# Routed experts visited once each, with half blocks and nested conditions, in a GNN and mixture-of-experts stack

## The chip, the cores and the metric

The kernel runs on one core of a Trainium2 chip. The core has a tensor engine (PE, with its weight loads shown apart as PEld), a vector engine (DVE), a scalar engine (ACT), GpSimd (POOL) and a sync engine (SP), each with an instruction queue of its own. The metric is the device time of one execution in microseconds, taken as the median of some runs. The kernel before took 1725.51 us (three runs, 1724.1 to 1725.95).

## The reference

The input is x, 625 nodes of 512 features, and a list of 10000 edges. Four graph layers alternate with four feed-forward layers, each added to x after a layer norm. Two of the feed-forward layers, called L1 and L3 here, are routed: each node picks two of eight experts, and only these two count in its sum. Cut to what matters:

```
# L1: 512 -> 1024 -> 512, with biases
logits = x @ gate_w + gate_b
vals, idx = top_k(logits, 2);  w = softmax(vals)
out = sum over the two experts e:  w_e * (relu(x @ w1[e] + b1[e]) @ w2[e] + b2[e])

# L3: 512 -> 1536 -> 512, gated
probs = softmax(x @ router_w.T)
gates, idx = top_k(probs, 2);  gates = gates / sum(gates)
out = sum over the two experts e:  gates_e * ((silu(x @ w1[e].T) * (x @ wgate[e].T)) @ w2[e].T)
```

So 1250 pairs of node and expert are computed in each of the two layers. All is float32. On the inputs of this case the experts get these numbers of nodes: in L1 96, 346, 175, 23, 54, 50, 350, 156, and in L3 197, 240, 352, 99, 77, 43, 149, 93.

## The kernel before

The whole stack is one straight program, scheduled by the order in which it is written: each engine takes its instructions in that order, and semaphores hold one behind another. x stays in on-chip memory as five groups of 125 nodes. The change touches the two routed layers and one place ahead of L1.

A routed layer starts with the logits. `top2` finds the two experts of each node as one-hot rows. `dispatch` (from L514) turns these into a list of places: matmuls with a triangle of ones give each pair its rank within its expert and each expert its total; a chain of small DVE instructions makes from rank and total a block number and a place in the block; one-hot matrices (`ohp` for the place, `ohb` for the block) ten matmuls then write the node of each place, and ten more its weight. There are NB = 17 blocks of B = 128 places: the first eight hold the first 128 nodes of each expert, the other nine ("overflow") hold what is left of the experts with more, in order. Empty places point to spare rows behind the nodes.

`routed` (from L621) runs over the blocks. `fetch` (L667) gathers a block's 128 rows of x by an indirect DMA on POOL's queue, two blocks ahead, into one of three buffers. `enter` (L674) transposes them on PE. `ahead` does the up matmuls of one chunk of 512 hidden features (L1170 in L1, L1335 in L3; 4 matmuls a weight chunk, each two instructions of 512 columns), `turn` (L688) transposes the hidden rows back, `back` (L697) multiplies by the down weights, scales by the weight of each place (L703) and adds the rows into `sums` in HBM by an indirect DMA (L705) on POOL. L1 has two chunks a block, L3 three. `run` orders them in a pipeline over the units (block, chunk) of all blocks: the up matmuls of the next unit stand between a unit's up matmuls and its turn, and its down matmuls come a unit later, across the border of two blocks as well. The eight base blocks are one such run; each overflow block is a run of its own, inside nested conditions `n_over > i`, so that after the first condition that fails all that follow are jumped over. The last thing in a run is the turn and the down matmuls of its last two units; the transposes of the next block (`enter`) stand ahead of these.

Weights come as chunks of 1 MB (128 x 2048 float32), four an expert in L1 and nine in L3, over a ring of eleven buffers on SP's queue (`bring`, `refill`, L206 and L730): as soon as a buffer has been read, the load of the chunk that is eleven further is issued. An overflow block loads its expert's chunks again, at an address that SP reads from the list of owners, under the condition that the block exists.

`fill` is a list of small pieces of work that `run` puts in, three a unit: in L1 the matmuls of the second bias (`expert_bias`, L479 and L486), the copy of x into `sums` (`keep`), and `normalise`, which makes the normalised adjacency for L2 out of the degrees with some 25 DVE instructions. L3 has only `keep`.

## Time and profile before

| what | value |
|---|---|
| median of three runs | 1725.51 us |
| the profiled execution: time, span | 1723.04 us, 1721.1 us |
| mean granted clock of PE | 0.936 |
| PE, DVE, ACT, POOL busy | 89%, 39%, 21%, 14% of the span |
| L1 routed: logits start, first up matmul, last down matmul ends | 771.3, 793.8, some 1018 us |
| L3 routed: softmax of the logits starts, first up matmul, last down matmul ends | 1259.9, 1282.2, some 1708 us |
| blocks run | L1: 8 and 6 overflow; L3: 8 and 5 overflow |
| bytes on SP's weight queue (q1) | 214.80 MB |

The columns of a row of instructions are: line, engine, operation, result and operands with the program's names and sizes, the number of instructions; busy time in all and mean length in nanoseconds of one; the idle time of the engine just before them, and what ended most of it. The chain is the work that ended last, followed back from the end. A row by stretches has, for each engine, busy time and number of instructions, then PE's granted clock as a share of full speed, the share of the DMA engines and the GB/s moved. Matmuls are pipelined, so the length of one is more than the distance to the next.

### The profile page before, as it was taken

To read this page: it belongs to the slowest core of one execution; us is meant where nothing else is said; L and a number is where in the kernel's file an instruction comes from. 1 tells how busy PE (TensorE), PEld (TensorE's weight loads), DVE (VectorE), ACT (ScalarE), POOL (GpSimd) and SP (SyncE) were. 2 spreads that over 40 slices of the span, in tenths; PEclk is the share of its full clock that TensorE was granted. 3 is DMA by queue.
4 is the path that set the end of the run, shared out by engine and by line. 5 is a ranking of instruction groups with operands and counts; after the bars stand their busy time and mean duration, and the time that the engine had idled before them with its cause. 6 is when DMAs were issued, how large, how long until landed. Compare 5 with 4: busy or idle time off the path is not lost.

```text
span 1721.1 us, 15559 instructions
## 1 busy us (share of the span) xinstructions
PE 1528.4 (89%) x5642; PEld 861.3 (50%) x5642; DVE 676.1 (39%) x1738; ACT 357.8 (21%) x680; POOL 235.5 (14%) x254
## 2 busy tenths in 40 slices
PE   7996999989897989846999969698759999999997
PEld 5774466555555656533444436354534444444443
DVE  9824562451974168466122225635331111111110
ACT  1102362011661046311111115301211000000100
POOL 2010042010540034101111112001000000000000
PEclk8998999999999989977999989799869999999998
DMA  3000200011001100136889731011258888869871
GB/s 135 16 28 25 73 1 25 31 68 53 22 1 49 49 26 1 40 112 234 302 270 342 256 87 73 25 49 49 102 217 299 301 309 304 307 244 359 311 265 50
DMA packets 40142, 237.12 MB, mean 138 GB/s; under 512 B 4779, under 2 KB 4907, under 8 KB 14299
## 3 DMA queue, kind: packets, MB, share of 16 engines
q1 hardware_dynamic: 30705, 214.80, 33.7%
q0 software_dynamic: 6608, 15.99, 4.1%
q10 hardware_dynamic: 2746, 5.25, 1.0%
q8 instruction: 48, 0.79, 0.2%
q14 instruction: 35, 0.29, 0.1%
HBM read 246.11 MB, written 14.26 MB: 151 GB/s over the span
## 4 chain that ended last, share of the span: by engine, by line
PE 70%; DVE 12%; issue 10%; DMA 4%; ACT 2%; POOL 1%; SPq 0%; POOLq 0%; ACTq 0%; DVEq 0%
PE ps_mf L359 17%; PE ps_y L697 9%; PE ps_h L1335 9%; PE ps_mn L367 7%; PE ps_h L1170 5%; PE ps_s L796 4%; PE ps_eo L496 4%; PE ps_o L860 3%; DMA sumsL<-slots,node 3%; PE ps_p L839 3%; PE ps_tr L328 2%; DVE ln_st L277 1%; DVE s L802 1%; PE ps_t L688 1%; DVE dst L913 1%
## 5 line engine op out<-in xcount | busy, mean ns | idle before, releaser
L1335 PE MATMUL ps_h<-ring,xgT 128*128 128x512 f32 x624 | 274.8, 595 | 0.8 <-DVE xgT L226 0.8
L697 PE MATMUL ps_y<-ring,hT 128*128 128x512 f32 x536 | 239.2, 593 | 0.9 <-issue 0.9
L1335 PEld LDWEIGHTS ps_h<-ring,xgT 128*128 128x128 f32 x624 | 118.7, 191 | 147.9 <-issue 145.3
L697 PEld LDWEIGHTS ps_y<-ring,hT 128*128 128x128 f32 x536 | 97.6, 190 | 103.9 <-issue 103.0
L825 POOL TENSOR_SCALAR s<-s,rs 125x625 f32<-125x625 f32 (+4 forms) x120 | 103.2, 875 | 294.0 <-DVE rs L822 269.9
L705 POOL DMA_INDIRECT sumsL<-slots,node x27 | 42.6, 1578 | 469.3 <-DVE slots L703 358.6
L1338 ACT ACTIVATE g<-ps_h 128x512 f32<-128x512 f32 x39 | 23.3, 597 | 395.6 <-PE ps_h L1335 364.5
L1170 PE MATMUL ps_h<-ring,xgT 128*128 128x512 f32 x224 | 103.2, 609 | 2.1 <-ACT xgT L234 1.3
L807 ACT ACTIVATE s<-s,mn 125x626 f32<-125x626 f32 (+4 forms) x120 | 87.2, 743 | 49.3 <-DVE mn L802 49.1
L802 DVE CUSTOM_DVE_ANT_0 s<-ps_s,mask 125x626 f32<-125x626 f32 (+4 forms) x120 | 82.6, 718 | 29.0 <-PE ps_s L796 27.8
L796 PE MATMUL ps_s<-kT,qT 64*125 64x313 f32 (+4 forms) x416 | 86.4, 466 | 2.8 <-DVE mn L802 2.8
L328 PE MATMUL ps_tr<-ident,xn 125*128 125x125 f32 x140 | 30.2, 398 | 62.6 <-DVE ln_nb L300 49.1
L226 DVE COPY hT<-ps_t 128x512 f32<-128x512 f32 x26 | 18.0, 692 | 171.5 <-PE ps_t L688 171.5
L1340 DVE TENSOR_TENSOR h<-ps_h,g 128x512 f32<-128x512 f32 x39 | 26.8, 686 | 147.9 <-ACT g L1338 147.9
L839 PE MATMUL ps_p<-ident,s 125*125 125x125 f32 x432 | 65.8, 293 | 14.0 <-POOL s L825 11.7
L359 PE MATMUL ps_mf<-xT,w 128*128 128x313 f32 x256 | 69.7, 434 | 6.6 <-ACT xT L402 6.6
L839 PEld LDWEIGHTS ps_p<-ident,s 125*125 125x125 f32 x432 | 53.9, 194 | 40.0 <-POOL s L825 28.6
L1170 PEld LDWEIGHTS ps_h<-ring,xgT 128*128 128x128 f32 x224 | 43.6, 196 | 57.5 <-issue 53.8
L817 DVE SCALAR_TENSOR_TENSOR s<-s,cnt 125x626 f32<-125x626 f32 x80 | 67.3, 863 | 9.9 <-ACT s L807 9.9
L496 PE MATMUL ps_eo<-w,h 128*125 128x512 f32 x160 | 70.6, 592 | 0.0
L860 PE MATMUL ps_o<-pT,v 125*64 125x375 f32 (+2 forms) x448 | 60.1, 413 | 9.0 <-DVE mn L802 4.2
L916 PE MATMUL ps_a<-dst,src 125*128 125x313 f16 x400 | 58.0, 309 | 6.9 <-DVE dst L913 5.3
(345 smaller groups left out, 1994.8 us busy)
## 6 DMA issues: line engine op xcount, KB each, us to landing
ring<-in_weights SPq DMA_DIRECT2D x195, 1024.0 KB
w<-in_weights SPq DMA_DIRECT2D x27, 1024.0 KB
rows_hbm<-xn ACTq DMA_DIRECT2D x2, 1120.0 KB
sumsL<-x ACTq DMA_DIRECT2D x2, 1120.0 KB
out<-sumsL SPq DMA_DIRECT2D x1, 1250.0 KB
x<-in_x SPq DMA_DIRECT2D x1, 1120.0 KB
x<-sumsL SPq DMA_DIRECT2D x5, 224.0 KB
rows<-in_rows SPq DMA_DIRECT2D x1, 1052.0 KB
```

The costliest lines, as they stand in the source:

```text
L359: nc.tensor.matmul(ps[:, half, :HC], w, r[:, half * HC:(half + 1) * HC], start=(n == 0), stop=(n == last))
L367: nc.tensor.matmul(ps[:T, 0, :width], src[:, k, t * T:(t + 1) * T], w[:, k, :width], start=(k == 0), stop=(k == KD - 1 and extra is None))
L496: nc.tensor.matmul(ps[:T, 0, :], h[:, t * T:(t + 1) * T], w, start=(f == 0), stop=(f == len(blocks) - 1))
L697: nc.tensor.matmul(ys[b][:, 0, :], hT[:, j, :], ring[n % RING][:, j, :], start=(c == 0 and j == 0), stop=(c == nch - 1 and j == 3))
L796: nc.tensor.matmul(ps[hh][:T, i, :w], qT[rr, b, t * T:(t + 1) * T], kT[rr, b, i * w:(i + 1) * w], start=True, stop=True)
L802: nc.vector.tensor_tensor_reduce(s[:, hh, :nb * w].rearrange("p (a c) -> p a c", a=nb), ps[hh][:T, :nb, :w], mask[:, t, :nb * w].rearrange ...
L807: nc.scalar.activation(s[:, hh, :nb * w], s[:, hh, :nb * w], AF.Exp, bias=mn[:, hh:hh + 1], scale=-1.0, accum_out=sm[:, hh:hh + 1] if caus ...
L825: nc.gpsimd.tensor_scalar(s[:, hh, :w], s[:, hh, :w], rs[:, hh:hh + 1], 1.0, op0=OP.mult, op1=OP.mult)
L839: nc.tensor.transpose(pp[:T, hh, j * T:(j + 1) * T], s[:, hh, j * T:(j + 1) * T], ident[:T, :T])
L860: nc.tensor.matmul(po[rr, 0, o:n * T], v[:, j, h * DH:(h + 1) * DH], pT[:, hh, j, o:n * T], start=(j == 0), stop=(j == nk - 1))
L1170: nc.tensor.matmul(ps[:, 0, :], xgT[:, k, :], w1[:, k, :], start=(k == 0), stop=(k == KD - 1))
L1335: nc.tensor.matmul(ps[:, i, :], xgT[:, k, :], w[i][:, k, :], start=(k == 0), stop=(k == KD - 1))
```

## The change

Experts are visited once each, in order, with no overflow list. The slots of an expert are now six (NL): slot 0 is a half block of 64 places, slots 1 to 5 whole blocks of 128. An expert whose number of halves (64 nodes, rounded up) is odd runs slot 0 for its first 64 nodes; then slot 1 runs if it has more than 64 nodes, and slots 2 to 5 in nested conditions. So NB is 48 for the places.

The half block (`Block` with l = 0) uses two column groups of the tensor engine: 64 nodes times the first half of the output columns go to the upper 64 rows of PSUM, the same nodes times the second half to the lower 64. Its result rows are added to `sums` as half rows, with their own list of places (`node2`, `gate2`).

Each block now runs its pipeline alone (`run`). Weights are loaded once an expert. The ring has twelve buffers; a refill during a block is issued under the condition that this block is the last of its expert, and every block of an expert starts from the same state of the ring. In L3 the order of an expert's chunks is up 0, gate 0, up 1, gate 1, down 0, up 2, gate 2, down 1, down 2, where before the three down chunks came last. The first twelve loads are issued ahead of the dispatch.

The rows of slots 1 and 0 of the next expert are gathered while one expert runs, into one buffer each (`fetch`, after `enter` has transposed the ones before); the rows of slots 2 and up go to a third buffer, and are transposed at the start of their block. Before expert 0, `enter(0)` and `enter(1)` stand one behind the other.

The dispatch has no thresholds, overflow numbers and owners; it has the totals, whether the halves are odd, and the start of the places. In L3 the softmax over eight is left out, and the two weights come from the difference of the two logits, as in L1. The bias matmuls of L1 move into the dispatch, behind the gather; their result is added to x there. `keep` follows the dispatch. `normalise` moves to the second layer of the graph layer ahead (two pieces after each evacuation of its projections).

The diff, cut to its core:

```diff
-TMORE = 3
+TMORE = 4
...
-NB = 17
-NO = NB - E
+NL = 6
+NB = E * NL
+BH = B // 2
...
-        for c in range(3):
-            w += [a[c], g[c]]
-        w += _chunks(i["L3_ffn_w2"][e].T)
+        d = _chunks(i["L3_ffn_w2"][e].T)
+        w += [a[0], g[0], a[1], g[1], d[0], a[2], g[2], d[1], d[2]]
...
+    def choose(lg):
+        m1, m2, o12 = top2(lg)
+        g12 = small.tile([T, 2, NT], F32, tag="g12", name="g12")
+        def weights12():
+            nc.vector.tensor_sub(g12[:, 1], m2, m1)
+            nc.scalar.activation(g12[:, 1], g12[:, 1], AF.Exp)
+            nc.vector.tensor_scalar(g12[:, 0], g12[:, 1], 1.0, None, op0=OP.add)
+            nc.vector.reciprocal(g12[:, 0], g12[:, 0])
+            nc.vector.tensor_mul(g12[:, 1], g12[:, 1], g12[:, 0])
+        return o12, g12, weights12
+    def dispatch(layer, lg, xg, bias=None):
...
+            weights12()
+            if bias is not None:
...
+            ci = dp.tile([P, E], I32, tag="ci", name="ci")
+            nc.vector.tensor_scalar(ci, tot, 1.0, float(BH - 1), op0=OP.max, op1=OP.add)
+            odd = dp.tile([P, E], I32, tag="odd", name="odd")
+            nc.vector.tensor_scalar(odd, ci, BH, None, op0=OP.bitwise_and)
+            base = dp.tile([P, E], F32, tag="base", name="base")
+            nc.vector.scalar_tensor_tensor(base, odd, -2.0, e768, op0=OP.mult, op1=OP.add)
...
-            gt = dp.tile([P, E, 4], F32, tag="gt", name="gt")
-            nc.vector.tensor_tensor(gt, tot[:, :, None].to_broadcast([P, E, 4]),
-                                    thr[:, None, :].to_broadcast([P, E, 4]), op=OP.is_gt)
-            nov = dp.tile([P, E], F32, tag="nov", name="nov")
-            nc.vector.tensor_reduce(nov, gt, axis=AX.X, op=OP.add)
-            pm = dp.tile([P, E, E], F32, tag="pm", name="pm")
-            nc.vector.tensor_mul(pm, before, nov[:, None, :].to_broadcast([P, E, E]))
-            ovb = dp.tile([P, E], F32, tag="ovb", name="ovb")
-            nc.vector.tensor_reduce(ovb, pm, axis=AX.X, op=OP.add)
-            delta = dp.tile([P, E], F32, tag="delta", name="delta")
-            nc.vector.scalar_tensor_tensor(delta, ovb, float(B), dconst, op0=OP.mult, op1=OP.add)
...
+            xg(node)
+            routing[layer] = number_of.rearrange("p a e -> p (a e)")
+            nc.vector.tensor_copy(number_of[:, 0, :], tot[0:1, :])
+            nc.vector.tensor_copy(number_of[:, 1, :], odd[0:1, :])
+            if bias is not None:
+                added = ktile("added")
+                for t in range(NT):
+                    if t % 2 == 0:
+                        pb = pstile("ps_eb")
+                    nc.tensor.matmul(pb[:T, t % 2, :], cT[:, t * T:(t + 1) * T], bias, start=True,
+                                     stop=True)
+                    nc.scalar.copy(added[:, t, :], pb[:T, t % 2, :])
 
...
+            firsts = dp.tile([P, 2, E], F32, tag="firsts", name="firsts")
+            for i, a in enumerate((node, gate)):
+                nc.vector.tensor_copy(firsts[:, i],
+                                      a.rearrange("p (e l) -> p e l", l=NL)[:, :, 0])
+            ps = pstile("ps_hf")
+            for g in range(2):
+                nc.tensor.matmul(ps[g * BH:(g + 1) * BH, 0, :2 * E], ident[:, :BH],
+                                 firsts.rearrange("p i e -> p (i e)"), start=True, stop=True)
+            node2 = small.tile([P, E], I32, tag="node2", name="node2")
+            nc.vector.tensor_scalar(node2, ps[:, 0, :E], 2.0, upper, op0=OP.mult, op1=OP.add)
+            gate2 = small.tile([P, E], F32, tag="gate2", name="gate2")
+            nc.vector.tensor_copy(gate2, ps[:, 0, E:2 * E])
+            if bias is not None:
+                for t in range(NT):
+                    nc.vector.tensor_add(x[:, t, :], x[:, t, :], added[:, t, :])
+        return node, gate, node2, gate2
...
+            rows_g = kpool.tile([P, NT, D], F32, tag="K", name="rows_g")
+            xg_half, xg_block, xg_more = rows_g[:BH, 0, :], rows_g[:, 1, :], rows_g[:, 2, :]
+            y_out = [rows_g[:, 3 + n, :] for n in range(2)]
+            xhT = [rpool.tile([P, KD, BH], F32, name=f"xhT{n}") for n in range(2)]
+            xbT = [rpool.tile([P, KD, B], F32, name=f"xbT{n}") for n in range(2)]
...
+            def refill(cond=None):
+                while brought["n"] < E * per:
+                    n = brought["n"]
+                    if n >= RING and n - RING not in read:
+                        return
+                    load(ring[n % RING], weights[w0 + n], cond)
+                    brought["n"] += 1
...
+            def fetch(e, node):
+                if e < E:
+                    gather(xg_block, node, e, 1)
+                    gather(xg_half, node, e, 0)
+            refill()
+            node, gate, node2, gate2 = dispatch(layer, lg, lambda node: fetch(0, node), bias)
+            _, numbers = nc.values_load_multi_w_load_instructions(routing[layer], min_val=0,
+                                                                  max_val=N)
+            counts, odd = numbers[:E], numbers[E:]
+            for part, hbm in by_node(sums[layer]):
+                nc.scalar.dma_start(hbm, x[part])
...
+            def turned(src, dst):
+                pt, n = pstile("ps_x"), src.shape[0]
+                for k in range(KD):
+                    nc.tensor.transpose(pt[:, 0, k * n:(k + 1) * n], src[:, k * P:(k + 1) * P],
+                                        ident[:n, :n])
+                evac(dst.rearrange("p k s -> p (k s)"), pt[:, 0, :KD * n])
+            def enter(e):
+                if e < E:
+                    turned(xg_block, xbT[e % 2])
+                    turned(xg_half, xhT[e % 2])
+                    fetch(e + 1, node)
...
+            class Block:
+                def __init__(self, e, l):
+                    self.e, self.l, self.h, self.hT = e, l, {}, {}
+                    n = 1 if l else 2
+                    self.parts = [(slice(g * B // n, (g + 1) * B // n),
+                                   slice(g * 512 // n, (g + 1) * 512 // n)) for g in range(n)]
+                    self.width = 512 // n
+                    self.xT = (xbT if l else xhT)[e % 2]
+                    self.cond = counts[e] < B * l + BH + 1 if l < NL - 1 else None
+                def done(self, i):
+                    read.add(self.e * per + i)
+                    refill(self.cond)
+                def ahead(self, c):
+                    ps, n = pstile("ps_h"), self.width
+                    for i, w in enumerate(up[c]):
+                        w = chunk_of(self.e, w)
+                        for k in range(KD):
+                            for rr, cc in self.parts:
+                                nc.tensor.matmul(ps[rr, i, :n], self.xT[:, k, :], w[:, k, cc],
+                                                 start=(k == 0), stop=(k == KD - 1))
...
+                def back(self, c):
+                    if c == 0:
+                        self.y = pstile("ps_y")
+                    hT, w, n, nj = self.hT.pop(c), chunk_of(self.e, down[c]), self.width, \
+                        self.width // P
+                    for g, (rr, _) in enumerate(self.parts):
+                        for j in range(nj):
+                            for ro, co in self.parts:
+                                nc.tensor.matmul(self.y[ro, 0, :n], hT[:, j, rr],
+                                                 w[:, g * nj + j, co],
+                                                 start=(c == 0 and g == 0 and j == 0),
+                                                 stop=(c == nch - 1 and g == len(self.parts) - 1
+                                                       and j == nj - 1))
+                    self.done(down[c])
+                    if c == nch - 1:
+                        if self.l == 0:
+                            i = self.e
+                            give(self.y[:, 0, :n], n, gate2[:, i:i + 1], by_half,
+                                 node2[:, i:i + 1])
+                        else:
+                            i = self.e * NL + self.l
+                            give(self.y[:, 0, :n], n, gate[:, i:i + 1], sums[layer],
+                                 node[:, i:i + 1])
+                def run(self):
+                    read.clear()
+                    read.update(before[0])
+                    brought["n"] = before[1]
+                    for n in range(nch + 2):
+                        if n < nch:
+                            self.ahead(n)
+                        if 1 <= n <= nch:
+                            self.turn(n - 1)
+                        if n >= 2:
+                            self.back(n - 2)
+            def more(e, l):
+                if l < NL:
+                    with tc.If(counts[e] > B * l - BH):
+                        turned(xg_more, xbT[e % 2])
+                        if l + 1 < NL:
+                            gather(xg_more, node, e, l + 1)
+                        Block(e, l).run()
+                        more(e, l + 1)
+            enter(0)
+            for e in range(E):
+                before = set(read), brought["n"]
+                enter(e + 1)
+                with tc.If(odd[e] > 0):
+                    Block(e, 0).run()
+                with tc.If(counts[e] > BH):
+                    gather(xg_more, node, e, 2)
+                    Block(e, 1).run()
+                more(e, 2)
...
-    normalise()
-    routed("L1", node, gate, 2, 1, l1_hidden, l1_turned,
-           expert_bias(comb, b2s[:E, 1, :]), fill)
+    routed("L1", lg, ((0,), (1,)), (2, 3), vec("L1_ffn_b1"), b2s[:E, 1, :])
...
-    pr = softmax8(node_logits(xnT, vec("L3_ffn_router_w"), None, "lg"))
-    m1, m2, o12 = top2(pr)
-    g12 = small.tile([T, 2, NT], F32, tag="g12", name="g12")
-    nc.vector.tensor_add(g12[:, 0], m1, m2)
-    nc.vector.reciprocal(g12[:, 0], g12[:, 0])
-    nc.vector.tensor_mul(g12[:, 1], m2, g12[:, 0])
-    nc.vector.tensor_mul(g12[:, 0], m1, g12[:, 0])
-    node, gate, whose = dispatch("L3", o12, g12.rearrange("p c t -> p (c t)"), W_L3, 9)
...
-    routed("L3", node, gate, 3, 2, l3_hidden, l3_turned)
+    lg = node_logits(xnT, vec("L3_ffn_router_w"), None, "lg")
+    routed("L3", lg, ((0, 1), (2, 3), (5, 6)), (4, 7, 8))
```

## The prediction

> **What bounds the kernel now.** I read the page's busy shares first, then the chain that ended last by stage, then the stretches between named instants. In the profiled execution (span 1721.1 us, time 1723.04; the median of the three runs is 1725.51, so its own sum gets 2.5 us more at the end) the tensor engine is the bound.
>
> ```profile
> PE 1528.4 (89%) x5642; PEld 861.3 (50%) x5642; DVE 676.1 (39%) x1738; ACT 357.8 (21%) x680; POOL 235.5 (14%) x254
> PE 70%; DVE 12%; issue 10%; DMA 4%; ACT 2%; POOL 1%; SPq 0%; POOLq 0%; ACTq 0%; DVEq 0%
> L1335 PE MATMUL ps_h<-ring,xgT 128*128 128x512 f32 x624 | 274.8, 595 | 0.8 <-DVE xgT L226 0.8
> L697 PE MATMUL ps_y<-ring,hT 128*128 128x512 f32 x536 | 239.2, 593 | 0.9 <-issue 0.9
> L1170 PE MATMUL ps_h<-ring,xgT 128*128 128x512 f32 x224 | 103.2, 609 | 2.1 <-ACT xgT L234 1.3
> q1 hardware_dynamic: 30705, 214.80, 33.7%
> q8 instruction: 48, 0.79, 0.2%
> ```
>
> The routed matmuls have almost no idle time: 0.8, 0.9 and 2.1 us in all. 624 up matmuls at 48 a block are 13 blocks in L3, 224 at 16 are 14 in L1: eight base blocks each, five and six overflow blocks. So a block less is its whole time gained, and any wait put on PE is its whole time lost. The stages, with columns PE, PE loads, DVE, ACT, POOL, clock, DMA share and rate:
>
> ```profile
> 794.00:925.00 131.00, 129.01 (x367) 61.46 (x368) 37.47 (x78) 18.33 (x45) 17.10 (x14) 0.98 0.86 298
> 925.00:1018.00 93.00, 92.05 (x266) 43.93 (x264) 21.32 (x63) 13.16 (x33) 15.50 (x12) 1.00 0.64 219
> 1282.00:1545.00 263.00, 262.85 (x705) 123.09 (x706) 31.61 (x48) 22.96 (x40) 17.60 (x14) 0.99 0.83 295
> 1545.00:1709.00 164.00, 163.42 (x441) 76.24 (x439) 21.11 (x31) 14.27 (x25) 12.91 (x10) 1.00 0.73 259
> ```
>
> Weights stream at 83 to 86% of the DMA engines while PE is full: a load is hidden only as long as nobody waits for all of them. From q1, 33.7% of 1721 us moves 214.80 MB, so a 1.05 MB chunk takes 2.83 us at full rate. The chain in L3 and at its start, and PE's first rows there (start, length, what, idle before):
>
> ```profile
> 1320.00 6.87 PE ps_h L1335 x16
> 1352.66 6.87 PE ps_h L1335 x16
> 1272.42 7.72 DMA slots<-rows_hbm,node
> 1280.28 1.09 PE L674 MATMUL ps_x<-ident,slots 128*128 128x128 f32 x4 [8.46 <-DMA slots<-rows_hbm,node]
> 1282.15 10.35 PE L1335 MATMUL ps_h<-ring,xgT 128*128 128x512 f32 x20 [0.78 <-DVE xgT L226]
> 793.79 5.33 PE L1170 MATMUL ps_h<-ring,xgT 128*128 128x512 f32 x8 [0.85 <-DVE xgT L226]
> 791.85 1.09 PE L674 MATMUL ps_x<-ident,slots 128*128 128x128 f32 x4 [4.57 <-DMA slots<-rows_hbm,node]
> 771.27 2.33 PE L421 MATMUL ps_lg<-xnT,lg_w 128*64 128x313 f32 x16 [0.63 <-ACT xnT L234]
> ```
>
> An L3 block is 1352.66 - 1320.00 = 32.7 us. A warm 8-matmul group takes 3.43 us (0.43 each), but 5.33 after the idle of 4.57, and 20 take 10.35 instead of 8.6 after 8.46: **an idle of some 5 us also costs about 1.8 us of slow clock** behind it. An idle of 0.8 does not.
>
> **The change, part by part.** Tokens per expert, from the reference's routing of these inputs: L1 96 346 175 23 54 50 350 156, L3 197 240 352 99 77 43 149 93. In halves of 64: L1 2 6 3 1 1 1 6 3, L3 4 4 6 2 2 1 3 2. After, L1 runs 9 full and 5 half blocks, L3 11 full and 2 half.
>
> *Half block.* Two 64-column groups replace one of 128. The row of L421 is the nearest: 64-wide, 313 columns, 16 matmuls in 2.33 us, 0.146 each, where one alone is 0.26 by the 0.43 of 512; two go side by side. So I take half of a full block (L3 16.4, L1 7.6); the bound on the other side is a whole one.
> 1. Blocks: L1 11.5 for 14, at 15.2 us: **-38**. L3 12 for 13: **-32.7**. This is all that the half blocks buy.
> 2. The expert-bias matmuls leave PE's path in L1 (0.7 + 1.98 + 2.77 us, with their waits and the gap of 1.28): **-6**; they now lie in the dispatch, in the gather wait (4.57 us idle today), and the cost is 0 to +3 if they overrun it. I take 0.
> 3. Shorter dispatch. L3 loses softmax8 (1259.92 to 1261.35, 1.4 us) and both lose a row of DVE steps of 0.14 to 0.23 us, but NB grows from 17 to 48, so ohb and gates lengthen: L3 **-3**, L1 0 (between -3 and +2).
> 4. The normalise steps (some 15 us of DVE) move out of L1's fill into layer 1's projections, where PE is full and DVE has room for two steps behind each 3.5 us group: 0, up to +5 if not.
>
> *What it adds on PE's path.*
> 5. Second gather. enter(1) stands ahead of expert 0's blocks on PE, but fetch(1) goes out on POOL only after enter(0) has read its buffer; before, three buffers let fetch(0) and fetch(1) go together. One more issue-to-landing per layer: 5.24 + transposes and evacuation, **+7.5** in L1; 7.72 in L3 with weights in flight, **+8** (bounds 5.2 and 10).
> 6. Blocks l=2 and up: gathered rows are transposed and evacuated at the block's start with nothing beside it: 0.7 to 0.9 evacuation idle, and an ACT table load (1.28 us) on the Relu/Silu alternation, some 1.8 each. L1 4, L3 4: **+7 and +7** (3 to 10).
> 7. Blocks no longer overlap their neighbours. In L1 (two chunks) the last turn waits for h (0.7) behind one 0.43 group, and back(0) for hT: 0.5 for each of 9 full, 1 for each of 5 half blocks, **+9.5**. L3 has a third chunk between: 0.
> 8. Entries are run for every expert, used or not: 8 half transposes, three unused whole ones: **+4 and +2**.
> 9. **The untaken half waits for the weights.** In the built program the skipped branch on SP brings its semaphores up to date by waiting for each load in flight, and PE's first matmul of the full block that follows waits for SP's bump, since the skipped half could have rewritten its ring slots. In L3 the last block of an expert issues nine loads; d0 is read only at 24.9 of 32.7 us, and five leave from there on: 25.1 + 5 x 2.85 + some 2 to land is 41, against a block end of 32.6. Less the entry transposes PE stands 8 us. e1 to e4: **+32**. Before, the same loads were hidden since they belonged to the next expert's third chunk. e5 (half only) reaches such chunks 3 us early, and its nine loads (26 us) outlast its visit, so e6 stands 11 us: **+14**. L1 loads four a visit; only e1 is caught: **+4**. Bounds: 0, if the wait is satisfied in time, and +50.
> 10. Short visits of L1's e3, e4, e5 (8.5 us): the next gather sits on POOL behind this expert's scatter-add (1.6 us issue, landing 6.6), then two gathers at 1 us and 5.3 to land, some 14 a round: **+11** (0 to 16).
> 11. Slow-clock restarts behind the idles of 5, 9 and 10: 4 in L1, 6 in L3 at 1.8: **+7 and +11**.
> 12. Skipped branches on PE, 14 in L1 and 15 in L3. Each drains PE's counter (matmul latency some 0.3 us) and jumps. Before, all Ifs that PE ran fell through, and cost nothing in the chain; the one skip per layer lies behind the last block, where POOL's next instruction came 0.1 us later. I take 0.7: **+10 and +10.5** (bounds 0.1 and 3, the latter if the code must be fetched).
>
> [...]
>
> Sum, L1: -38 - 6 + 7.5 + 7 + 9.5 + 4 + 4 + 11 + 7 + 10 = **+16**. L3: -32.7 - 3 + 8 + 7 + 2 + 32 + 14 + 11 + 10.5 = **+49**. The profiled execution becomes 1788, the median 1790 us.
>
> **Rivals.**
> A. *Faster: the skipped branch does not hold PE.* If the loads land before the skip's bump is wanted (item 9 nothing, 6 of the restarts gone) and skips cost 0.1: -50 - 11 - 18 on the sum, -14: **1711**. For it: DMA share 0.83, not 1, and fewer chunks in all (104 loads instead of some 170). Against it: nine loads of 2.83 need 25.5 us of 32.7, and five are bound to the tail. It decides when the stall per expert is under 1 us.
> B. *Code is fetched at each skip.* A small load lands in some 3 us (the 256 KB fills: 3.0), 29 skips at 3 instead of 0.7: +67, **1857**. For it: PE's program nearly doubles. [...]
> C. *Halves do not run side by side.* Five times 7.6 and two times 16.4: +71, **1861**. Against: L421.
>
> **How the numbers follow.** Sum as worked out 0.57 (own range 1755 to 1825); A with its partial forms 0.26; B 0.12; C 0.05. The range goes from 1702 (A with the gather chain of 10 hidden too) to 1850 (most of B). Within 0.2%, 3.5 us, which is also about what a measurement here can tell from no change, falls 0.04, from partial forms of A. Faster 0.22, slower 0.74.
>
> **What would show it.** Right: PE idle of 6 to 10 us before ps_h at e1 to e4 of L3, ended by a DMA of ring or by SP's queue; a second idle before ps_x at each stage's start; clock under 1 behind them; half blocks of 16 and 8 us; fewer bytes on q1 (some 140 MB). Wrong: L3's routed stretch (now 1282.15 to 1708.4, 426 us) under 400 says A; more than 480 with idle at skips ended by nothing named says B; ps_h rows of half blocks at 0.43 a pair of columns instead of 0.21 says C. The largest single doubt is item 9, then 12.

## The result, and the profile after

The changed kernel took 1797.82 us (median of four runs, 1795.88 to 1803.73) against 1725.12 us for the kernel before: 1.0427 times as long, 95% interval 1.0402 to 1.0453. The forecast was 1790 us, range 1702 to 1850, slower with a chance of 0.74. The profiled execution took 1799.03 us and its span was 1797.2 us, 76 us more than the span before. Below, e0 to e7 are the experts of a layer, and an expert that runs its half block alone (e3, e4 and e5 of L1, e5 of L3) is called half-only.

The page of the changed kernel, lines that answer to those of before (L761 are the up matmuls of both layers, L718 the transposes at an expert's entry):

```profile
PE 1512.9 (84%) x5966; PEld 861.8 (48%) x5966; DVE 671.3 (37%) x1697; ACT 382.2 (21%) x709; POOL 256.5 (14%) x275
...
q1 hardware_dynamic: 20769, 142.44, 21.3%
...
q8 instruction: 85, 1.39, 0.3%
...
L761 PE MATMUL ps_h<-ring,xbT 128*128 128x512 f32 x672 | 318.7, 633 | 62.1 <-SPq L847 40.2
...
L718 PE MATMUL ps_x<-ident,rows_g 128*128 128x128 f32 (+1 forms) x160 | 25.9, 302 | 40.6 <-PEq L836 25.8
```

PE works 15.5 us less than before, and the weight queue moves 72 MB less: 142 MB, where some 140 were forecast. But the up matmuls, which had 2.9 us of idle time ahead of them in all, now have 62, and the entry transposes 41. 40.2 of the first are ended by SP's queue at L847, the condition around the half block; 25.8 of the second by PE's own sequencer at L836, the condition around further blocks.

The stretch from first to last routed weight matmul of each layer, changed kernel (columns PE, PE loads, DVE, ACT, POOL, clock, DMA share, GB/s):

```profile
806.50:1035.90 229.40, 197.98 (x764) 98.41 (x764) 39.27 (x91) 27.63 (x78) 39.80 (x36) 0.92 0.42 130
1301.10:1783.70 482.60, 419.27 (x1288) 198.26 (x1288) 51.23 (x81) 61.45 (x85) 38.51 (x32) 0.92 0.42 148
```

The same stretches before:

```profile
793.80:1018.00 224.20, 221.26 (x631) 105.59 (x631) 58.99 (x141) 31.48 (x78) 32.81 (x26) 0.99 0.77 265
1282.10:1708.40 426.30, 426.25 (x1144) 199.33 (x1144) 52.08 (x77) 37.23 (x65) 30.42 (x24) 1.00 0.79 282
```

PE now stands 31 us in L1 and 63 in L3, and the mean clock of both stretches has fallen from 0.99 and 1.00 to 0.92.

Cut at the logits (first L421 of the layer), the first up matmul and the last down matmul, the whole difference is:

| stretch | before | after | difference |
|---|---|---|---|
| up to L1's logits | 771.3 | 772.5 | +1.2 |
| L1 logits to first up matmul | 22.5 | 34.0 | +11.5 |
| L1 weight matmuls | 224.2 | 229.4 | +5.1 |
| L1's end to L3's logits | 235.4 | 234.1 | -1.4 |
| L3 logits to first up matmul | 28.7 | 31.2 | +2.5 |
| L3 weight matmuls | 426.3 | 482.6 | +56.3 |
| rest | 12.7 | 13.5 | +0.9 |

L1 together is +16.6 (forecast +16), L3 +58.8 (forecast +49).

Who PE waited for in the two stretches of weight matmuls, changed kernel, L3 and then L1 (us in all, times, longest):

```profile
PE ps_h L761 <- SPq L847: 36.6, 4, 9.4
PE ps_x L718 <- PEq L836: 11.6, 4, 7.2
PE ps_h L761 <- PEq L847: 10.6, 2, 5.5
PE ps_h L761 <- ACT xbT L234: 4.1, 4, 2.0
PE ps_h L761 <- SPq L836: 3.3, 1, 3.3
...
PE ps_x L718 <- PEq L836: 14.2, 3, 7.8
PE ps_h L761 <- SPq L847: 3.6, 1, 3.6
```

Four waits for SP in L3, 36.6 us: these are e1 to e4, the forecast's item 9 (32 us). But 38.6 us in the two layers (11.6, 10.6 and 14.2 in these lines, and 2.2 before one ps_h of L1) are ended by PE's own sequencer, where the sum had 20.5 us for the skipped branches on PE (item 12). The place of the first wait for SP, at e1 of L3, PE's rows and then the instructions of line L847 there:

```profile
1370.81 0.59 PE L804 MATMUL ps_y<-ring,hT 128*128 128x512 f32 x1
1373.05 1.02 PE L718 MATMUL ps_x<-ident,rows_g 128*128 128x128 f32 x8 [1.64 <-PEq L836]
1382.66 2.04 PE L761 MATMUL ps_h<-ring,xbT 128*128 128x512 f32 x2 [8.60 <-SPq L847]
```

```profile
L847 SPq EVENT_SEMAPHORE  x8: 17/17/17, 1382.1 to 1382.6; - x8
L847 PEldq COMPARE_BRANCH  x1: 6470/6470/6470, 1373.2 to 1373.2; - x1
L847 DVEq COMPARE_BRANCH  x1: 63/63/63, 1374.1 to 1374.1; - x1
...
L847 PEldq EVENT_SEMAPHORE  x1: 51/51/51, 1379.7 to 1379.7; - x1
L847 SPq COMPARE_BRANCH  x1: 50/50/50, 1381.9 to 1381.9; - x1
```

SP comes to its branch only at 1381.9 and brings its semaphores up to date by 1382.6; PE goes on at 1382.66. That is the forecast wait. What SP did just before, from 1364 to 1384:

```profile
SPq L836 <- SPq L836: 9.6, 5, 3.7
```

So the waiting for loads is done at L836, in the skipped nest of further blocks of e0, and L847, the skipped half block of e1, passes the delay on in 0.7 us. But PE's own branch, which DVE does in 63 ns, takes **6470 ns** there. It lies under the wait for SP and is hidden by it. At e6 nothing hides it: there the rows of L836 have

```profile
L836 PEldq COMPARE_BRANCH  x1: 6598/6598/6598, 1682.6 to 1682.6; - x1
...
  PE ps_x L718: 7.2, 1
```

and PE stands 7.2 us. In the trace's DMA records two packets of 16 KB of the instruction queue q8 start at 1684.84 and 1686.11, inside this branch, two at 1375.48 and 1376.80 inside the one at e1, and one at 1298.27 inside a branch of 4.35 us at L3's start. Of PE's 80 branches in the two layers, 18 have such a packet inside, and they take 2.5 to 7.1 us; one takes 1.4 without; the other 61 take 0.07 to 0.44. So the long branches wait for code. Distance alone does not decide it: the jump over the half block of L3 takes 6.47 us at e1 and 0.35 at e3.

The half blocks do what they should. PE's rows for one in L1, and the start of a whole block behind it:

```profile
883.95 3.67 PE L761 MATMUL ps_h<-ring,xhT 128*64 128x256 f32 x32
887.56 0.44 PE L777 MATMUL ps_t<-ident,h 128*128 128x128 f32 x2
888.14 0.44 PE L777 MATMUL ps_t<-ident,h 128*128 128x128 f32 x2
888.51 3.67 PE L804 MATMUL ps_y<-ring,hT 128*64 128x256 f32 x32
892.12 3.27 PE L761 MATMUL ps_h<-ring,xbT 128*128 128x512 f32 x7
```

It takes 892.12 - 883.95 = 8.2 us, against the 15.2 of the forecast for a whole one.

### The profile page after: what moved, and what is told of

The parts are those of the page before. It is cut to its first block, busy times and chain, and to the rows that moved or that the text cites. A ratio compares the mean times of both kernels' runs of the same rounds, so it can differ in the third digit from the quotient of the medians.

```text
span 1797.2 us, 17215 instructions
## 1 busy us (share of the span) xinstructions
PE 1512.9 (84%) x5966; PEld 861.8 (48%) x5966; DVE 671.3 (37%) x1697; ACT 382.2 (21%) x709; POOL 256.5 (14%) x275
## 5 line engine op out<-in xcount | busy, mean ns | idle before, releaser
L761 PE MATMUL ps_h<-ring,xbT 128*128 128x512 f32 x672 | 318.7, 633 | 62.1 <-SPq L847 40.2
L761 PEld LDWEIGHTS ps_h<-ring,xbT 128*128 128x128 f32 x672 | 134.1, 204 | 227.2 <-issue 216.1
L804 PE MATMUL ps_y<-ring,hT 128*128 128x512 f32 (+1 forms) x664 | 209.8, 511 | 0.0
L804 PEld LDWEIGHTS ps_y<-ring,hT 128*128 128x128 f32 (+1 forms) x664 | 92.7, 169 | 92.2 <-issue 83.4
L733 POOL DMA_INDIRECT sumsL<-rows_g,node x27 | 43.1, 1598 | 581.2 <-DVEq L836 299.2
L769 DVE TENSOR_TENSOR h<-ps_h,g 128x512 f32<-128x512 f32 (+1 forms) x39 | 25.2, 647 | 249.3 <-ACT g L768 249.3
L694 POOL DMA_INDIRECT rows_g<-rows_hbm,node x52 | 50.3, 967 | 150.0 <-DVE gates L628 72.1
L732 DVE TENSOR_SCALAR rows_g<-ps_y,gate 128x512 f32<-128x512 f32 (+1 forms) x27 | 18.4, 681 | 137.0 <-PE ps_y L804 137.0
L359 PEld LDWEIGHTS ps_mf<-xT,w 128*128 128x128 f32 x256 | 49.5, 194 | 26.6 <-ACT xT L402 7.1
L718 PE MATMUL ps_x<-ident,rows_g 128*128 128x128 f32 (+1 forms) x160 | 25.9, 302 | 40.6 <-PEq L836 25.8
## 6 DMA issues: line engine op xcount, KB each, us to landing
x<-sumsL SPq DMA_DIRECT2D x5, 224.0 KB
```

The costliest lines, as they stand in the source:

```text
L359: nc.tensor.matmul(ps[:, half, :HC], w, r[:, half * HC:(half + 1) * HC], start=(n == 0), stop=(n == last))
L761: nc.tensor.matmul(ps[rr, i, :n], self.xT[:, k, :], w[:, k, cc], start=(k == 0), stop=(k == KD - 1))
L804: nc.tensor.matmul(self.y[ro, 0, :n], hT[:, j, rr], w[:, g * nj + j, co], start=(c == 0 and g == 0 and j == 0), stop=(c == nch - 1 and g = ...
```

## The experiments

Theory 1 is item 9 of the prediction: SP's skipped half block holds PE until the weights in flight have landed. Theory 2 came from the profile after: a taken branch on PE waits for its code. A theory 3 came later: both hold, and the loads in flight lengthen the fetch of code. The rivals are that the time lies in the work added around the blocks, and, for L1, that gathers come late (item 10). Times are medians; differences are to the changed kernel's 1797.8 us; ratios are to the kernel before on the same chip, whose medians on the chips used were 1724.4 to 1726.0 us.

### The half block behind the first whole block

```diff
-                with tc.If(odd[e] > 0):
-                    Block(e, 0).run()
                 with tc.If(counts[e] > BH):
                     gather(xg_more, node, e, 2)
                     Block(e, 1).run()
-                more(e, 2)
+                with tc.If(odd[e] > 0):            # now odd + (tot > 128)
+                    with tc.If(odd[e] > BH // 2):
+                        Block(e, 0).run()
+                    more(e, 2)
```

(and the condition of the loads, so that the last block of an expert issues them.)

> Same work, other order: the half block of an expert stands behind its first whole block, and the skips of half block and further blocks are joined where both are empty. Theory 1 (PE waits at e1 to e4 of L3 because SP's skipped half block first lets all weight loads land): the first chunks of an expert are no longer touched by a block that can be skipped just ahead of them, so the idles of 8.6, 9.4, 9.4 and 9.2 us go, e5 (half only) gets such a wait instead of its 3.3. Theory 2 (the taken branch on PE itself takes 3 to 7 us where its target must be fetched): most branches now stand behind the last matmuls of a block, which are queued ahead and cover them, so the idles of 5.5 at e0 and 5.1 at e7 go too. Both together: 45 to 55 us less than the changed kernel, some 1745 us. Rival (the time is in separate block pipelines and entries): under 10 us less.

1756.63 us, 41 less, where 45 to 55 were expected; ratio 1.0177 (1.0156 to 1.0199). Idle in L3's stretch fell from 63.3 to 31.9 us. The four waits for SP at e1 to e4 are gone, e5 has one of 9.1 as expected, and e7 one of 5.0 that was not expected. L1 did not gain (32.8 us idle): its half-only experts now jump over the whole block instead. The order alone takes back more than half of the loss. It does not tell theory 1 from 2, since both go with the order.

### A shorter nest

```diff
-NL = 6
+NL = 4
```

> Four slots an expert instead of six: the code that is jumped over behind an expert's last block shrinks from four whole blocks to two. On these inputs no expert has more than 352 nodes, so nothing is left out here; an expert with over 448 would lose nodes. Theory 2 (code fetch): the long branches behind L1's e3 and e4 (3.8 and 7.1 us) and L3's e5, e6 and e7 (6.6, 6.6 and 3.2) shorten by a page of code or go, 10 to 25 us less than the changed kernel. Theory 1 (weights landing) and the chain of gathers: nothing changes but 1 us of the dispatch.

1769.06 us, 29 less, where theory 2 had 10 to 25; ratio 1.0244 (1.0218 to 1.0270). No work that was done before is left out. L1's stretch went from 229.4 to 215.4 us: the idles before ps_x that PE's sequencer ended fell from 14.2 to 7.3. L3's went from 482.6 to 470.2; the waits for SP at e1, e2 and e4 stayed (8.8, 9.3 and 10.3 us), and the branch at L3's start too (4.1 us). The wait at e3 fell from 9.4 to 1.2 us, which neither theory had foreseen, and most of L3's gain is there. The trace has the reason: e2 of L3 has three whole blocks, and with four slots the third is the last, so that its loads carry no condition and no nest is skipped behind it. SP comes to L847 at 1549.0, 0.6 us after PE's last down matmul of e2; with six slots it came at 1575.9, 10.8 us after, from a skipped nest. PE goes on at 1550.9, and only at 1553.7 has SP seen the last load land. So the skipped half block alone does not hold PE until all loads have landed; the skipped nest ahead of it does. Code packets fell from 85 to 72. So L1's idle at its half-only experts goes with the code that is jumped over, and is not the chain of gathers of item 10, which this run leaves as it was.

### No loads from blocks

```diff
                 def done(self, i):
                     read.add(self.e * per + i)
-                    refill(self.cond)
```

> The loads that blocks issue are left out in both layers, so that only the first twelve chunks of a layer are loaded and later experts multiply by the wrong weights; every instruction on PE stays. Theory 1 alone: the idles before ps_h at L3's e1 to e4 fall under 1 us, and with them e5's 3.3, e6's 7.2 and L1's 3.6; some 60 to 70 us less. Theory 1 and 2: what is left is the branch, 6.5 to 7 us at e1, 5 at e2, 1 at e3, 5.5 at e4, and e6 stays at 7; some 25 to 30 us less.

1705.88 us (one run), 92 less, more than either theory allows. But L1's output is another one, so L3's routing is too, and L3 ran other blocks; only L1 can be read. There the wait for SP (3.6 us) is gone, the longest branch is 3.9 us instead of 7.1, and the stretch is 217.1 us instead of 229.4. The same was then done in L3 alone:

```diff
-                    refill(self.cond)
+                    if layer == "L1":
+                        refill(self.cond)
```

> As the run without loads from blocks, but in L3 alone, so that L1 computes the right thing and L3's routing is that of the reference; L3 multiplies by wrong weights from its second expert on. Idle inside L3's routed stretch is 63 us in the changed kernel. Theory 1 alone (weights landing): the waits of 8.6, 9.4, 9.4, 9.2 and 3.3 us fall under 1 us each, e6 and e7 too, 50 us of idle less and some 65 us of time. Theory 1 and 2 (a fetch of code at the branch of 3 to 7 us, whatever the loads do): 21 us of idle less, some 25 us of time. Theory 3 (both, and the weight loads lengthen the fetches, since both go through the DMA engines): branches of 3 to 4 us instead of 5 to 7, 35 us of idle less, some 40 us of time.

1752.70 us (one run), 45 less; idle in L3 went from 63.3 to 22.7 us. Of the three numbers that of theory 3, some 40 us less, is the nearest. At e1 PE's rows are now, with the branch of L848 (L847 of the changed kernel) behind them:

```profile
1374.09 1.02 PE L718 MATMUL ps_x<-ident,rows_g 128*128 128x128 f32 x8 [1.10 <-DVEq L837]
1376.77 3.61 PE L762 MATMUL ps_h<-ring,xbT 128*128 128x512 f32 x4 [1.67 <-ACTq L848]
```

```profile
L848 PEldq COMPARE_BRANCH  x1: 453/453/453, 1374.2 to 1374.2; - x1
```

Both waits have gone from this place, for SP and for code: 0.45 us instead of 6.47. Theory 1 is shown. Theory 3 can be read where both kernels fetch one packet at the same branch, the nest skipped behind the whole blocks of L3's e0, e1, e3 and e6. At e0, changed kernel and then this one:

```profile
L836 PEldq COMPARE_BRANCH  x1: 6969/6969/6969, 1365.3 to 1365.3; - x1
L837 PEldq COMPARE_BRANCH  x1: 3769/3769/3769, 1366.9 to 1366.9; - x1
```

At the four places the branch takes 6.6 to 7.0 us in the changed kernel and 3.4 to 3.8 here. By the DMA records the packet itself takes 0.9 to 1.4 us in both, but it starts 4.1 to 4.6 us after the branch there and 0.9 to 1.1 here. From e0's branch to its packet the DMA engines are 93% busy there, and 6% here. So at these places the fetch is longer with loads in flight. Whether a branch fetches at all is another thing: that of e1 above is free here with no change to PE's work, and the runs do not show why.

### The old order of L3's weights

```diff
-        w += [a[0], g[0], a[1], g[1], d[0], a[2], g[2], d[1], d[2]]
+        w += [a[0], g[0], a[1], g[1], a[2], g[2], d[0], d[1], d[2]]
...
-    routed("L3", lg, ((0, 1), (2, 3), (5, 6)), (4, 7, 8))
+    routed("L3", lg, ((0, 1), (2, 3), (4, 5)), (6, 7, 8))
```

> L3's chunks of an expert again in the order up, gate three times and then the three down chunks, as in the kernel before. Six loads instead of four leave before the down matmuls, so the last lands some 4 us earlier, about 37.5 us after the block's start instead of 41. Theory 1: the waits for SP at e1 to e4 fall from 9 to about 5 us each, but not under the length of the branch (6.5, 4.8, 0.4, 5.3 us) where theory 2 holds: 12 to 16 us less than the changed kernel. If the loads in flight are not what PE waits for: nothing.

1771.17 us, 27 less; ratio 1.0269 (1.0241 to 1.0297); the expectation was 12 to 16. The idles before e1 to e4 are 5.3, 7.1, 4.8 and 4.6 us where they were 8.6, 9.4, 9.4 and 9.2: 14.8 less, as worked out from the landing of the last load. The first, 5.3, is PE's branch (5.6 us) and not SP. What was not foreseen: e5's wait (3.3) and most of e7's (5.1 to 1.7) went too, and with less idle came less slow clock: the time on a lowered clock in L3's stretch fell from 74 to 43 us.

### Loads behind the expert, out of all conditions

```diff
                 def done(self, i):
                     read.add(self.e * per + i)
-                    refill(self.cond)
...
                 more(e, 2)
+                read.update(range(e * per, (e + 1) * per))
+                refill()
```

> The changed kernel with its weight loads taken out of the conditions: they are issued without a condition behind each expert, so no branch of SP has a load in it. All work is done with the right weights, and the order on PE is that of the changed kernel. Theory 1: nothing on PE can wait for SP's skipped branch any more, and in L3 the chunks still come in time, since the first of nine lands some 5 us after an expert's end and is read 10 us after it. Theory 2: what is left at L3's e1, e2 and e4 is the branch itself (6.5, 4.8 and 5.3 us), at e3 1 us, at e6 7. Some 20 to 25 us less than the changed kernel, about 1775, and by the weights alone (without theory 2) 1745 or less. If the loads, which now leave in one burst beside the branches, lengthen the fetches, the gain falls to 15.

1762.42 us, 35 less, where 20 to 25 were expected; ratio 1.0213 (1.0197 to 1.0229). All weights are loaded and used, and SP has no load in a condition. PE's waits in L3's stretch:

```profile
PE ps_h L760 <- PEq L846: 14.1, 2, 7.1
PE ps_x L718 <- PEq L835: 6.1, 1, 6.1
PE ps_h L760 <- DMA ring<-in_weights: 6.1, 3, 4.1
PE ps_x L718 <- DVEq L835: 5.5, 5, 1.1
```

None is for SP. So the waits of e1 to e4 were for SP's skipped blocks, and not for the weights themselves, which come in time for all but e5 and e6 (6.1 us). What is left is code: e3 and e4, where the branch over the half block now stands beside the burst of loads and takes 7.1 and 7.5 us, while e1 and e2 are free. The nests skipped behind the whole blocks of e0, e1, e3 and e6, where now no load is in flight, take 3.3 to 3.7 us.

### Whole blocks only

```diff
-            nc.vector.tensor_scalar(odd, ci, BH, None, op0=OP.bitwise_and)
+            nc.vector.tensor_scalar(odd, ci, 0, None, op0=OP.bitwise_and)
...
-                with tc.If(odd[e] > 0):
-                    Block(e, 0).run()
-                with tc.If(counts[e] > BH):
-                    gather(xg_more, node, e, 2)
-                    Block(e, 1).run()
+                gather(xg_more, node, e, 2)
+                Block(e, 1).run()
```

(with the conditions moved by half a block, and no gather or transposes for a half.)

> The change without its half blocks: an expert runs its first whole block without any condition and further ones under nested conditions, 14 blocks in L1 and 13 in L3 as before the change; no half block is gathered, transposed or jumped over. Blocks: +38 in L1 and +33 in L3 against the changed kernel. If theories 1 and 2 hold, what the jump over the half block costs goes with it: e0 5.5, e1 to e4 36.6, e5 to e7 some 12, slow clock behind these 15, L1 some 15, half entries 4: 88 less. Together some 15 to 20 us less than the changed kernel: the half blocks, as they are put in, cost more than they save. Rival (the half blocks earn their 71 us and the loss is elsewhere): 50 to 70 us more.

1756.72 us, 41 less; ratio 1.0177 (1.0160 to 1.0194); 15 to 20 less were expected. With 14 and 13 blocks again, L1's stretch is 236.2 us and L3's 440.5, and they are almost full:

```profile
803.50:1039.70 236.20, 218.42 (x610) 101.61 (x608) 42.42 (x91) 30.25 (x76) 39.59 (x35) 0.99 0.47 139
1300.80:1741.30 440.50, 427.79 (x1138) 197.44 (x1136) 52.23 (x77) 36.51 (x64) 36.81 (x30) 1.00 0.46 162
```

```profile
PE ps_x L717 <- DVEq L834: 6.6, 6, 1.1
PE ps_h L759 <- DVE xbT L226: 5.0, 5, 1.0
PE ps_x L717 <- DMA rows_g<-rows_hbm,node: 3.8, 1, 3.8
```

No wait for SP, none for code (the nests' branches, 6.0 to 6.5 us in most of L3, lie under the block's last matmuls), clock 0.99 and 1.00. The half blocks save 3.5 blocks and cost more than that: without them the kernel is 41 us faster. The rest of the change costs 31 us against the kernel before: 26 in the stretches (+12 and +14: 1.1 us behind each skipped nest, 1.0 before each further block, and blocks that no longer overlap), 9 on the way to L1's first block, less 4 on the way to L3's.

### The early gathers of expert 1

```diff
-                    gather(xg_block, node, e, 1)
-                    gather(xg_half, node, e, 0)
+                    gather(rows_of(e)[0], node, e, 1)     # expert 1: two buffers of its own
+                    gather(rows_of(e)[1], node, e, 0)
```

> The gathers for expert 1 go to two buffers that are free at the start, right behind those for expert 0, so that both land together. By the prediction's working the second gather costs 7.5 us in L1 and 8 in L3: 15 us less than the changed kernel. By the trace of the changed kernel PE stands 4.6 us in L1 and 3.2 in L3 for it, and in L3 the branch behind it takes 4.3 us whatever comes before: 8 to 10 us less.

1788.96 us, 9 less, as expected from the trace; ratio 1.0362 (1.0336 to 1.0388). The way from logits to first up matmul fell from 34.0 to 29.4 us in L1 and from 31.2 to 28.4 in L3. Item 5 had the right cause and was too large: 7.4 us in the two stretches instead of 15.5.

### Together

```diff
+                        if n == nch and 0 < self.l < NL - 1:
+                            turned(xg_more, xbT[e % 2])      # inside the block ahead
```

(this, with the half block behind, four slots, the old weight order and the early gathers.)

> Together: half block behind the first whole block with joined skips, four slots an expert, L3's weight order of before, the early gathers of expert 1, and the transposes for a further block moved into the block ahead of it, between its last turn and its down matmuls. From 1757 of the first of these alone: 9 for the gathers, 7 for the transposes (eight idles of 0.7 to 2 us), 15 to 20 for the short nest in L1 and at L3's e5 and e6, 4 to 8 for the weight order: some 1715 to 1722, under the kernel before.

1729.44 us, 68 less; ratio 1.0020 (1.0008 to 1.0031): almost the kernel before, and short of the expectation. L1's half-only experts still waited 12.5 us for SP, L3's e5 and e7 9.5. With the loads behind the expert as well:

> The combined kernel (1729.4) with its loads behind each expert, out of all conditions. The waits for SP that it still had (5.5 and 7.1 us at L1's e3 and e4, 4.4 at L3's e5, 5.1 at e7, and four of 1.1 to 1.4) fall to the branches under them, 2 to 3 us where there is one; L3's e5 may wait some 3 us for a chunk. With the slow clock behind these idles 12 to 18 us less than the combined kernel: 1711 to 1718, under the kernel before.

1722.31 us; ratio 0.9990 (0.9981 to 0.9999). Only 7 of the 12 to 18 came, because in L1 a new wait took the place of the old:

```profile
PE ps_x L722 <- DMA rows_g<-rows_hbm,node: 20.1, 4, 8.5
```

The loads alone were changed, and in the combined run the same line was

```profile
PE ps_x L722 <- DMA rows_g<-rows_hbm,node: 2.1, 2, 1.1
```

The four loads of an expert now leave in one burst, and the gathers of rows come late beside them. L3 gained as expected (433.4 to 424.0 us), L1 lost (220.3 to 224.0). The same with six slots:

> The same with six slots an expert, so that any routing is computed: the code jumped over behind an expert is longer again. By theory 2 some 5 to 12 us more than with four slots, at the half-only experts of L1 and at L3's e5 and e6, where a half block's few queued matmuls do not cover the fetch: 1718 to 1728.

1747.27 us; ratio 1.0126 (1.0111 to 1.0142): 25 more than with four slots, over twice the 5 to 12 that were expected. L1's stretch is 242.3 instead of 224.0 us. Four idles there of 2.4 to 4.4 us (one of them ended by a weight load) lie at branches on PE that take 3.2 to 5.5 us, which the short nest does not have, and the clock is lowered for 44.8 us instead of 27.7. L3's stretch is 5.5 us longer, with 2.5 at a branch before e7. The direction is that of theory 2; the size was put too low, in part because the slow clock behind each branch was left out.

Last, each layer with what suited it and four slots: L3 with the loads behind the expert, L1 with the half block first and the conditional loads of the changed kernel:

```diff
+                if layer == "L1":
+                    with tc.If(odd[e] > BH // 2):
+                        Block(e, 0).run()
+                    with tc.If(counts[e] > BH):
+                        gather(xg_more, node, e, 2)
+                        Block(e, 1).run()
+                    more(e, 2)
+                    continue
```

> The combined kernel in L3 (half block behind the first whole block, loads behind the expert, 424 us from first to last weight matmul, as measured there). In L1 the order and the conditional loads of the changed kernel instead (half block first), since with the loads in bursts L1's gathers came late (idles of 6.5, 8.5 and 4.7 us before ps_x) and the short nest alone had L1 at 215.4 us against 224.0. The early transposes take some 3 off that: 212 in L1. Four slots an expert and the early gathers stay. From 1722 some 12 less: 1708 to 1714, 0.8% under the kernel before. If the late gathers come from the early fetch or the early transposes instead, L1 stays at 220 and over: 1719 or more.

**1708.74 us; ratio 0.9893 (0.9873 to 0.9914)**: faster than both kernels, by 17 us than the one before and by 89 than the changed one. Its stretches, from an execution of 1713.88 us, the longest of the four:

```profile
805.20:1014.50 209.30, 192.39 (x776) 96.38 (x776) 40.49 (x94) 27.41 (x78) 37.39 (x33) 0.95 0.45 139
1275.10:1698.40 423.30, 407.99 (x1312) 195.61 (x1312) 51.22 (x82) 60.89 (x88) 37.51 (x31) 0.98 0.47 167
```

209.3 and 423.3 us against 224.2 and 426.3 before. The four slots limit it to experts with at most 448 nodes; these inputs have 352.

## Why the prediction was right, and where it was not

The sign, the size (1790 for 1798) and the largest single cause were right. Part of the agreement is luck: three items (9 at e6, 10 and 12) were wrong in their cause and others in their size, and they cancel.

- **Item 1, blocks (-38, -32.7).** Right: a half block takes 8.2 us in L1 (7.6 and a stall of 1 were put). In L3 (16.4) the one of e6 takes 19.6, 2.3 of it slow clock, so some 17.3 at full clock by its rows. Rival C is out.
- **Item 9, the wait for SP (+32, +4, e5 +3).** Right in cause and close in size: 36.6 us at e1 to e4, 3.6 in L1, 3.3 at e5. The loads behind the expert take all of the waiting for SP away, and the old weight order 14.8 of the 36.6, as worked out from landing times. One detail was off: at e1 SP waits for the loads in the skipped nest of the expert ahead, and the skipped half block only passes the delay on; where no nest was skipped (e3 with four slots) 1.2 us was left.
- **Item 9, e6 (+11).** Wrong. The 7.2 us there are PE's branch, 6.6 us, not loads.
- **Item 12, skips at 0.7 us (+10, +10.5), and rival B.** The 0.7 us was the author's estimate, one price for all skips, and no branch of PE in the changed kernel comes near it: 61 of the 80 take 0.07 to 0.44 us, one takes 1.4, and the 18 with a packet of q8 inside take 2.5 to 7.1. The kernel before has one such already: a branch of L730 that starts at 1702.35 takes 3.84 us, with a packet of q8 starting at 1703.85 inside it, and PE's last down matmuls of L3, which end at 1708.4, hide it. Rival B's price of 3 us was low for a branch that fetches (2.5 to 7.1), but many of these stand behind the last matmuls of a block, and PE's sequencer reaches them up to some 6 us ahead of PE: of 6.9 us at 1651.6, 1.5 are seen as idle. So PE's sequencer ends 38.6 us of idle in the two layers, where 20.5 were put, for another reason and at fewer places.
- **Item 10, gathers behind scatters in L1 (+11).** Wrong in cause, and near in size by luck: the idles at these experts (4.4, 7.8, 2.0 and 2.2 us, 16.4 in all) are branches, and the shorter nest alone takes 14 us off L1. The gathers cost 2.1 us in the combined kernel, and 20.1 only where the loads leave in a burst.
- **Item 11, slow clock (+7, +11).** Too small in L3: the first 32 up matmuls behind an idle of 5 us or more take 15.6 to 17.0 us instead of 14.0, and with e6 seven such places cost some 17 us.
- **Item 6, further blocks (+7, +7).** Half of it: eight idles of 0.7 to 2.0 us, 7.4 in all. The ACT table load that was put into each shows in one alone (1.28 us at 1336.99, in the idle of 2.0).
- **Item 7, blocks alone (+9.5).** Too large: the turn waits 0.3 to 0.4 us a block, some 3 us.
- **Item 5 (+7.5, +8).** 7.4 us together by the early gathers.
- **Item 2, bias matmuls in the gather's wait (0, at most +3).** At its upper bound or over: the ten wide bias matmuls ran at a clock of 0.50 (9.2 us), stood ahead of the matmuls for the weights, and held the first transposes until 796.9, some 3 us after the gather should have landed (788.3 and the 5.2 us of before).
- **Item 3, dispatch (0, -3).** In L3 better than put: with whole blocks only, the way from logits to the first up matmul is 24.8 us against 28.7 before, although it has the second gather. One reason is in the trace: the first gather, issued at 1285.56, is in by 1289.04; the one before took 7.72 us, with the DMA engines some 90% busy.
- **Item 4, normalise (0).** +1.2 us.

Behind each skipped nest PE stands about 1.1 us before the entry transposes, since DVE first scales the block's result (0.75 us) and then brings its semaphores up to date; the sum had this only within item 12.

Left open: why the same jump fetches its code in one kernel and not in another.

## What to carry to other kernels

A condition that is not taken was not free here: SP's false path waited for the loads that its queue had in flight (9.6 us at e1 of L3), and passed this wait on to PE, whose matmuls could have depended on the block (8.6 us of idle there). Loads belong outside of conditions (35 us less with the loads behind the expert), or the next block must not touch what the skipped one could have written (41 us less with the half block behind the first whole block). A jump on PE should stand behind a block's queued matmuls (1.5 us of idle behind a branch of 6.9 us at 1651.6), not ahead of the first one (5.5 us behind one of 4.35 at L3's start), and the code jumped over should be short (29 us less with the shorter nest). Where a jump fetched its code, it was shorter with no bulk load in flight (3.4 to 3.8 us against 6.6 to 7.0). What a smaller block saves has to be set against the jump over it (41 us less with whole blocks only). A fix that makes transfers leave in a burst has to be looked at for what else shares the DMA engines: here it was right for L3 (433.4 to 424.0 us) and wrong for L1 (220.3 to 224.0).

## What the runs showed that was not expected

- A branch on PE takes 2.5 to 7.1 us in the changed kernel where a 16 KB packet of code starts inside it, and all others but one take 0.07 to 0.44 us; one took 7.5 with the loads behind the expert, at 1588.4. At the four places compared above the packet starts 0.9 to 1.1 us after the branch with no weight load in flight, and 4.1 to 4.6 us after it with loads. The same conditions cost 34 to 76 ns on ACT, POOL and DVE in the changed kernel.
- PE's sequencer came to the skipped nests behind L3's whole blocks up to 13 matmul instructions, some 6 us, ahead of PE, so that a branch there is nearly hidden (of 6.9 us at 1651.6, 1.5 are idle). Behind a half block alone it is not: two skips follow each other there, and at e5 of L3 PE's sequencer brings the first one's semaphore up to date only at 1682.41, when the last matmul has ended (1682.36), so that the long branch starts at 1682.56.
- Two kernels that differ only in where SP's loads stand had their long branches over the half block at different experts (e1, e2 and e4 of L3 in one, e3 and e4 in the other).
- Taking one wait away showed the next below it at the same place twice: code under SP at e1 (old weight order, 5.3 us), weights under SP at e5 (loads behind the expert, 4.1).
